# Storing the convolution's parts from ScalarE's queue instead of GpSimd's in a graph network layer

## The chip, the cores and the metric

The kernel runs on one core of a Trainium2 chip. The metric is the device time in microseconds (us) of one execution. A profile is one execution recorded by the hardware profiler; times in it count from the start of its span. The engines are called by their names in the profile: PE is TensorE (matmuls), PEld its weight loads, DVE is VectorE, ACT is ScalarE, POOL is GpSimd and SP is SyncE. The last one computes nothing here: it issues DMA transfers.

## The reference

For each of 32 batches with 512 nodes and 256 channels, the layer normalises `x`, clips it at zero, and computes from the result `h`

```python
hc = relu(bn1(conv1(h)))                 # one tap, 256 to 256 channels
x_conv = relu(bn2(conv2(hc)) + h)        # 17 taps along the nodes
s = h @ w_se.T + b_se                    # 3 numbers per node
A = exp(-squared_distance(s)) * adj
x_nmp = A @ relu(h @ w_msg.T + b_msg)    # messages from the neighbours
# gates of a recurrent cell from [x_conv, x_nmp] and h: r, z, n
out = x + (1 - z) * n + z * h
```

Everything is 32-bit floating point. What matters here is `x_conv`, the convolution of 17 taps with its batch normalisation `bn2`: its values are what the changed stores carry.

## The kernel before, in words

The whole program is written out by a Python planner: there is no loop on the chip. Five generators (`rows`, `begins`, `graphs`, `conv`, `gates`) yield pieces of work; the main loop at the end of the kernel always takes the one whose clock is most behind, and so interleaves their matmuls in one fixed order on PE. The planner keeps an estimated time `now`, and an estimated time `free` for DVE and for ACT. Work that must come a little later than the piece that causes it goes into a list with a due time (`later`, line 158), which the main loop empties as `now` passes. These estimates decide only the order in which instructions stand on each engine. What an instruction waits for is found by the framework from the data that it reads and writes, and from the transfers' completion counters.

The five kinds of work are these:

- `begins`: loads a batch of `x`, normalises it on DVE and ACT, turns it so that channels lie on partitions, and stores it in DRAM as `hd`. From batch 8 on, turning goes by way of DRAM: a store to `xd` (line 928), eight loads that bring it back in blocks (line 907, called from `begin`), and two transposes on DVE into `hT` (line 938), which GpSimd stores to `hd` (line 942).
- `rows`: loads `hT` from `hd` (line 211), multiplies it by the weights of `conv1`, and writes the result to `h1`, the input of the long convolution.
- `conv`: the 17 taps, done as a fast convolution with 25 products for each of seven groups of batches (`STARTS`, line 36). Each product is a sum of matmuls into the PSUM tiles `ps_b` and `ps_c`. DVE prepares the operands (`x`, `xd`) and adds up the products (`n`, `z`, `y`). The weights `w` of the products come from DRAM for each group (line 570).
- `graphs`: masks (`m_sb`, lines 336 and 339), messages and distances, ending in the sums over the neighbours, which ACT copies out of PSUM as `right` and `at`, and which GpSimd stores in DRAM as `nd` (line 170).
- `gates`: for each batch, six products per half of the channels from `hTb` (line 225), `xconv` (line 231) and `xnb` (line 251), which are the batch's `h`, `x_conv` and `x_nmp` loaded again from DRAM, and then the gates on ACT and DVE. The result is added to `res`, a block of `x` (line 907, called from `load_res`), and stored (line 1078).

When the 25 products of a group are summed, `y` holds the group's convolution, and `EVAC` gets an entry for each batch in the group and each half of the channels. `evacuate` (line 677) takes these one at a time: ACT applies `bn2` and brings the columns into order in a tile `part`, of which there are three (line 687), and 0.4 us later by the planner's time a DMA stores it in DRAM, in the batch's `cd` (line 696, the line that the diff changes). From there `load_conv` (line 227) fetches it as `xconv` when the batch's gates are near. A group boundary need not be a batch boundary, so some batches are stored in two pieces. There are 72 parts in all, in seven bursts, one after each group.

DMA transfers are issued by three engines, each in the order of its own instruction stream. SP issues all loads (1254 transfers with a few last stores). GpSimd issues the stores of `hd`, `nd`, `xd`, `out`, of the third weights and, before the change, of `cd` (469 in all). ACT issues 29: the weights' stores at the start (line 561) and some of the last blocks of the output. [...]

Of the kernel before, what the change touches and what calls it, by code (L numbers as in the profile page):

```python
# [48 lines left out]
def kernel(  # L49
# [31 lines left out]
    nc = tc.nc  # L81
# [5 lines left out]
    def sizes(g):  # L87


        nu = STARTS[g + 1] - STARTS[g]  # L90
        return nu, ND * nu, 2 * ND * nu, ND * (nu + 1)
# [39 lines left out]
    dve, act = Engine(nc.vector, 0.12, 0.00108), Engine(nc.scalar, 0.16, 0.0009)  # L131
# [26 lines left out]
    def later(t, f):  # L158
        LATER.append((t, f))
        LATER.sort(key=lambda e: e[0])  # L160
# [28 lines left out]
    CD = {b: dram.tile([P, ND, N], F32, name=f"cd{b}") for b in range(B)}  # L189
# [487 lines left out]
    def evacuate():  # L677

        t, y, g, b, o = EVAC[0]
        if now < t or act.free > now + 0.3 or len(PARTS) > 2 and now < PARTS[-3]:  # L680
            return False
        EVAC.pop(0)
        nu, nh, _, _ = sizes(g)
        v0 = U * b - STARTS[g]
        first, last = max(0, -v0), min(U, nu - v0)
        c = o * nu + v0 + first
        part = late.tile([P, Q * U], F32, name="part", bufs=3)[:, : Q * (last - first)]
        act.activation(
            part.rearrange("p (u h k) -> p k h u", h=2, k=9),
            y.rearrange("p e f (h n) -> p (e f) h n", h=2)[:, :, :, c : c + last - first],  # L690
            AF.Identity, bias=bn2_sh[:, o : o + 1], scale=bn2_sc[:, o : o + 1],
        )
        act.free += 0.7
        PARTS.append(act.free + 5.0)
        n0, n1 = Q * first, min(Q * last, N)
        later(act.free + 0.4, lambda: nc.gpsimd.dma_start(CD[b][:, o, n0:n1], part[:, : n1 - n0]))
        if o == ND - 1 and last == U:
            evacuated[b] = PARTS[-1]
        return True
# [502 lines left out]
    def fill():  # L1202
        while LATER and LATER[0][0] <= now:
            LATER.pop(0)[1]()
        if EVAC:
            evacuate()
        while dve.free < now + 1.5 and background():
            pass
# [159 lines left out]
```

## Time and profile before

| | before |
|---|---|
| time, median of three (lowest to highest) | 2110.38 us (2107.77 to 2115.62) |
| span of the profiled execution | 2111.7 us |
| PE busy | 2058.5 us, 97% |
| DVE busy | 1512.7 us, 72% |
| ACT busy | 754.5 us, 36% |
| POOL busy | 339.9 us, 16% |
| mean granted PE clock | 0.993 |
| bytes moved by DMA | 383.07 MB, 181 GB/s |

Issuing a DMA counts as busy time on POOL, not on the other engines. The profile's view of the DMA issues gives, for each kind of transfer, its issuing engine, its size, and the median time from issue to landing. The ones near the change:

| transfer | issuer | count | KB each | median us to landing |
|---|---|---|---|---|
| `cd<-part`, full parts | POOL | 56 | 256 | 3.3 |
| `hd<-hT` | POOL | 32 | 512 | 5.9 |
| `wd<-w` | ACT | 25 | 512 | 4.2 |
| `xnb<-nd` | SP | 64 | 256 | 3.5 |
| `x_sb<-xd` | SP | 192 | 64 | 3.4 |
| `xconv<-cd` | SP | 32 | 512 | 5.5 |

The other sixteen stores of `cd` carry 81 to 175 KB. One issue of `cd<-part` takes 0.54 us on POOL, and from issue to landing the 72 of them took from 2.3 to 7.8 us.

To read the other views: a line of the waits names the engine and line that waited, what ended the wait, the total in us, the number of times and the longest. A line of the timeline gives the start, the duration, the engine and line, the operation with what it writes and reads, how often it stands in a row, and in brackets the idle time of the engine before it and what ended that.

### The profile page before, as it was taken

What the parts mean: (1) busy time and instruction counts of PE and PEld (TensorE: products, weight loads), DVE (VectorE), ACT (ScalarE), POOL (GpSimd) and SP (SyncE); (2) the same over time, 40 slices, a digit from 0 to 9 for tenths busy, and PEclk for the clock granted to TensorE, in tenths of its full rate; (3) what the DMA queues carried; (4) which work ended last, traced back from release to release, by engine and by line L of the source; (5) the groups of instructions that cost most, each with busy time, mean ns of one, the idle gap of its engine ahead of it and who ended that gap; (6) DMA issues with size and microseconds to landing.
All of it is one profiled execution on the core that took longest, in us unless ns stands there. A gap on an engine that the chain in (4) does not pass through costs nothing.

```text
span 2111.7 us, 25916 instructions
## 1 busy us (share of the span) xinstructions
PE 2058.5 (97%) x8774; PEld 1259.8 (60%) x8774; DVE 1512.7 (72%) x2660; ACT 754.5 (36%) x1267; POOL 339.9 (16%) x582
## 2 busy tenths in 40 slices
PE   9999799999999999999999999999999999999998
PEld 6887476664666556665466665456665666654443
DVE  6887598985898668877488866588985877763333
ACT  5553533226432263332443322533224432233111
POOL 2000112211201021111121101211111110112111
PEclk9999999999999999999999999999999999999999
DMA  7445787776966767676775767677766655624332
GB/s 282 167 149 190 258 252 202 202 206 181 244 186 204 221 170 199 182 184 194 215 185 177 192 189 198 181 185 211 210 177 190 188 155 165 170 72 109 86 90 40
DMA packets 546436, 383.07 MB, mean 181 GB/s; under 512 B 456576, under 2 KB 473472, under 8 KB 545664
## 3 DMA queue, kind: packets, MB, share of 16 engines
q1 hardware_dynamic: 512992, 282.17, 50.7%
q0 software_dynamic: 28624, 86.01, 11.9%
q10 hardware_dynamic: 4688, 13.24, 1.6%
q8 instruction: 70, 1.15, 0.2%
q14 instruction: 62, 0.51, 0.1%
HBM read 281.95 MB, written 99.35 MB: 181 GB/s over the span
## 4 chain that ended last, share of the span: by engine, by line
PE 63%; DMA 1%; issue 1%; DVE 1%; ACT 1%; POOL 0%; SPq 0%; DVEq 0%; ACTq 0%; POOLq 0%
PE ps_acc L136 37%; PE ps_g L136 11%; PE ps_c L136 9%; PE ps_b L136 4%; PE ps_b L867 1%; DMA hT<-hd 1%; ACT r L127 1%; PE ps_g L141 0%; DMA hd<-hT 0%; DMA m_sb<-in_adj_dram 0%; DVE y L127 0%; DVE r L127 0%; ACT at L127 0%; DVE z L127 0%; DVE right L127 0%
## 5 line engine op out<-in xcount | busy, mean ns | idle before, releaser
L136 PE MATMUL ps_acc<-hTb,whh 128*128 128x512 f32 x768 | 359.1, 599 | 18.0 <-ACT r L127 14.6
L136 PE MATMUL ps_acc<-xconv,wih 128*128 128x512 f32 (+1 forms) x772 | 362.0, 591 | 0.0
L136 PE MATMUL ps_acc<-xnb,wih 128*128 128x512 f32 (+1 forms) x772 | 358.9, 591 | 2.8 <-DMA xnb<-nd 2.8
L136 PEld LDWEIGHTS ps_c<-xd,w 128*128 128x128 f32 x2400 | 294.3, 191 | 31.7 <-issue 26.7
L136 PE MATMUL ps_c<-xd,w 128*128 128x135 f32 (+1 forms) x2400 | 303.7, 279 | 0.6 <-DVE z L127 0.3
L1078 POOL DMA_DIRECT2D out_dram<-res x252 | 164.6, 659 | 616.9 <-DVE res L127 520.9
L136 PEld LDWEIGHTS ps_acc<-hTb,whh 128*128 128x128 f32 x768 | 140.4, 190 | 179.8 <-issue 136.9
L136 PEld LDWEIGHTS ps_acc<-xnb,wih 128*128 128x128 f32 x772 | 142.9, 190 | 160.0 <-issue 154.2
L136 PEld LDWEIGHTS ps_acc<-xconv,wih 128*128 128x128 f32 x772 | 142.8, 190 | 156.9 <-issue 154.0
L136 PE MATMUL ps_g<-at,msg 128*128 128x512 f32 x512 | 227.2, 593 | 1.5 <-DVE at L127 1.5
L136 PEld LDWEIGHTS ps_b<-x,w 128*128 128x128 f32 x1200 | 157.0, 190 | 43.3 <-issue 37.3
L127 ACT ACTIVATE mid<-ps_b 128x270 f32<-128x270 f32 (+1 forms) x150 | 59.5, 396 | 344.9 <-PE ps_b L136 334.6
L127 DVE TENSOR_TENSOR r<-ps_acc,r 128x512 f32<-128x512 f32 (+1 forms) x65 | 44.2, 681 | 190.3 <-PE ps_acc L136 190.2
L136 PE MATMUL ps_b<-x,w 128*128 128x135 f32 (+1 forms) x1200 | 163.3, 278 | 0.7 <-ACT at L127 0.7
L136 PEld LDWEIGHTS ps_g<-at,msg 128*128 128x128 f32 x512 | 95.4, 190 | 112.4 <-issue 108.1
L127 DVE SCALAR_TENSOR_TENSOR x<-x,x 128x544 f32<-128x544 f32 (+5 forms) x161 | 137.7, 855 | 2.9
L136 PE MATMUL ps_g<-hT,w 128*128 128x512 f32 (+4 forms) x288 | 122.9, 573 | 15.5 <-DMA hT<-hd 11.5
L127 DVE TENSOR_TENSOR msg<-ps_g,bmsg 128x256 f32<-128x256 f32 x128 | 53.8, 421 | 108.1 <-PE ps_g L136 107.7
L127 ACT ACTIVATE z<-ps_acc,brz 128x512 f32<-128x512 f32 x64 | 44.0, 688 | 234.6 <-PE ps_acc L136 234.5
L127 DVE TENSOR_TENSOR x<-x 128x272 f32<-128x272 f32 (+5 forms) x280 | 127.6, 497 | 0.2
L136 PE MATMUL ps_g<-wmsg,hTg 128*128 128x259 f32 x496 | 124.1, 382 | 0.3 <-DVE aug L127 0.3
L127 DVE TENSOR_TENSOR xd<-x 128x544 f32<-128x544 f32 (+1 forms) x150 | 106.6, 718 | 23.9 <-PE ps_c L136 23.5
(121 smaller groups left out, 2591.9 us busy)
## 6 DMA issues: line engine op xcount, KB each, us to landing
w<-wd SPq DMA_DIRECT2D x125, 768.0 KB, 5.2
m_sb<-in_adj_dram SPq DMA_DIRECT2D x384, 64.0 KB, 3.2
hd<-hT POOLq DMA_DIRECT2D x32, 512.0 KB, 5.9
hT<-hd SPq DMA_DIRECT2D x32, 512.0 KB, 4.6
hTb<-hd SPq DMA_DIRECT2D x32, 512.0 KB, 5.5
xnb<-nd SPq DMA_DIRECT2D x64, 256.0 KB, 3.5
xconv<-cd SPq DMA_DIRECT2D x32, 512.0 KB, 5.5
res<-in_x_dram SPq DMA_DIRECT2D x256, 64.0 KB, 3.0
```

The costliest lines, as they stand in the source:

```text
L127: getattr(self.engine, name)(*tiles, **more)
L136: nc.tensor.matmul(ps, lhsT, rhs, **more)
L867: nc.tensor.matmul(pss[c], gr.left[k, :], gr.right[k, :], start=True, stop=True, tile_position=(32 * c, 0),)
L1078: queue.dma_start(OB[b][:, s.start // 32 : s.stop // 32, o * P + 32 * g : o * P + 32 * g + 32], y[at, s].rearrange("i (k j) -> i k j", j=32),)
```

## The change

The store of each part is issued by ACT, which also computes the part, and no longer by GpSimd:

```diff
         act.free += 0.7
         PARTS.append(act.free + 5.0)
         n0, n1 = Q * first, min(Q * last, N)
-        later(act.free + 0.4, lambda: nc.gpsimd.dma_start(CD[b][:, o, n0:n1], part[:, : n1 - n0]))
+        later(act.free + 0.4, lambda: nc.scalar.dma_start(CD[b][:, o, n0:n1], part[:, : n1 - n0]))
         if o == ND - 1 and last == U:
             evacuated[b] = PARTS[-1]
```

It is meant to take the stores out of GpSimd's queue, where they stand behind stores that wait for other work, and to let the engine that made a part send it off itself. The planner's times are not changed, so PE, DVE and SP keep the order of their instructions; ACT gets 72 DMA issues between its other instructions, and GpSimd loses as many.

## The prediction

> **What bounds the kernel now.** I read the page's first two parts, then the waits of TensorE, ScalarE and GpSimd, then the timeline around the stores that the diff touches. The page's busy row and TensorE's longest waits:
>
> ```profile
> PE 2058.5 (97%) x8774; PEld 1259.8 (60%) x8774; DVE 1512.7 (72%) x2660; ACT 754.5 (36%) x1267; POOL 339.9 (16%) x582
> ...
> PE ps_acc L136 <- ACT r L127: 14.6, 17, 1.8
> PE ps_g L136 <- DMA hT<-hd: 11.5, 5, 6.8
> ```
>
> TensorE is busy for 2058.5 of 2111.7 us; all its gaps together are 53 us. Its order is fixed, so the change can gain at most some gaps and can lose whatever makes a matmul late. GpSimd, which is relieved, is busy for 16%: of its waits, 147.7 us of the stores' own are for the part that they store.
>
> The stores come in bursts of about ten, one at each group's end: in the timeline between 236 and 285 us, then at 497, 752, 1028, 1333, 1624 and 1886. So I read the timeline of two bursts, and one earlier place where ScalarE already stores:
>
> ```profile
> 193.09 0.34 ACTq L561 DMA_DIRECT2D wd<-w  x1
> 193.48 0.56 ACT L127 ACTIVATE z<-ps_c 128x464 f32<-128x464 f32 x1 [0.41 <-ACT w L127]
> ...
> 760.91 0.95 SPq L251 DMA_DIRECT2D xnb<-nd  x2
> 761.96 5.24 SPq L907 DMA_DIRECT2D x_sb<-xd  x8
> 770.50 0.60 ACT L127 ACTIVATE at<-ps_g 128x512 f32<-128x512 f32 x1 [2.84 <-PE ps_g L136]
> 770.99 3.53 ACT L127 ACTIVATE part<-y,bn_shift,bn_scale 128x522 f32<-128x522 f32 x3
> 772.54 0.70 DVE L127 STREAM_TRANSPOSE hT<-x_sb 128x512 f32<-128x512 f32 x1
> 775.45 1.88 PE L136 MATMUL ps_acc<-xnb,wih 128*128 128x512 f32 x4
> ...
> 1342.97 3.78 PE L136 MATMUL ps_acc<-hTb,whh 128*128 128x512 f32 x4 [1.80 <-ACT r L127]
> 1359.80 7.43 SPq L907 DMA_DIRECT2D x_sb<-xd  x8
> 1368.21 0.70 DVE L127 STREAM_TRANSPOSE hT<-x_sb 128x512 f32<-128x512 f32 x1
> 1372.18 0.70 DVE L127 STREAM_TRANSPOSE hT<-x_sb 128x512 f32<-128x512 f32 x1
> 1373.18 0.54 POOL L942 DMA_DIRECT2D hd<-hT  x1 [1.17 <-DVE hT L127]
> 1373.49 0.69 ACT L127 ACTIVATE z<-ps_acc,brz 128x512 f32<-128x512 f32 x1 [2.32 <-PE ps_acc L136]
> 1383.27 1.40 PE L136 MATMUL ps_g<-hT,w 128*128 128x171 f32 x8 [0.33 <-DMA hT<-hd]
> ```
>
> Columns: start, time, engine, line, operation; in brackets the idle time before it. Note two things. SyncE's loads of `xnb` and `x_sb` are issued ten to fifteen microseconds before ScalarE makes the parts beside them: today SyncE runs ahead. And 1359.80 to 1383.27 is one chain: load of `x_sb`, two transposes, store to `hd`, load of `hT`, matmul, with 0.33 us of waiting left at its end.
>
> [...]
>
> **The change part by part.** *Removed:* 72 stores from GpSimd, 72 x 0.54 = 39 us of its time, none on TensorE's path: no matmul waits for GpSimd after the first microseconds. The `hd` store at 1373.18 waited for VectorE, not for a store ahead of it. I count 0.
>
> *Added on ScalarE:* 72 issues. Each leaves the engine idle for about 0.40 us (0.40 and 0.41 after the two stores at 187.82 and 193.09): 72 x 0.40 = 29 us into 1357 us of idle time. It matters only where ScalarE works without a pause up to something that TensorE awaits. That is so in the first burst: TensorE waits 0.67 us at 263.81 for the exponentials, and four stores now stand before them: 4 x 0.40 = 1.6 us. Elsewhere bursts end in idle time of 1 to 5 us: 0 to 1 us together.
>
> *Added waits.* This is the part that the diff does not show. I compared the two built programs, instruction by instruction with the semaphores that each awaits. The orders of TensorE, VectorE and SyncE are unchanged. But the DMAs of SyncE and ScalarE share eight completion counters, given out in turn, and each DMA first waits until the previous one on its counter has landed; GpSimd's have eight of their own. Moving 72 stores over makes them take turns with SyncE's loads, in both directions.
>
> Stores behind loads: for each store I compared the landing of the DMA before it on its counter with the time at which ScalarE arrives there. All 72 had landed, by 2.5 to 47 us. Nothing is added.
>
> Loads behind stores: 60 of SyncE's DMAs now wait for a part's store, and SyncE, held at one, holds all those behind it. Where SyncE ran ahead, this costs. Landing of a store: 3.3 us, the median of the 56 stores of 256 KB on GpSimd; of `xnb` 3.5 and `x_sb` 3.4.
>
> Burst at 752: the first `xnb` load follows a store that ScalarE reaches after `at` at 770.50 and two parts, some 2.43 us later: 773.4. It lands at 776.8, the `xnb` load at 776.8 + 3.5 = 780.3, and TensorE wants it at 775.45: **+4.8 us**. Next come eight loads of `x_sb`, behind two stores at about 774.8 (landed 778.1). The fourth, at 0.65 us each (5.24 for eight), lands at about 783.5, and VectorE, which needs it at 772.54, stands for 11 us. What is queued there: the sums of the next products, a read of `ps_c` at 781.46 among them, which TensorE needs only at 787.79, or 792.6 once it is itself 4.8 late. VectorE's own idle time of 2.2 us at 780.15 takes part of the 11, so this second delay hides: 0.
>
> Burst at 1333: the fourth of the eight `x_sb` loads follows a store that stands on ScalarE behind `z`, which awaits TensorE and ends at 1374.2. Landed at 1374.2 + 3.3 = 1377.5; four more loads at 0.65 and a landing of 3.4 put the eighth at 1383.5. The second transpose started at 1372.18: 11.3 us late, and the chain to the matmul at 1383.27 has no slack: **+11.3 us**. From both sides: with the shortest store landing, 2.3 us, it is 10; with the longest, 7.8, 16.
>
> Burst at 236: the last of eight `x_sb` loads follows a store after `right` (ends 261.95, now 1.6 later): landed 266.9, load landed at 270.3 to 272.1 against 269.68. The transpose and, 1.8 us behind it, the read of `ps_c` that TensorE awaits at 272.32 come up to 2.4 us later; with the 1.6 above, which overlaps, **+2.5 us**. Bursts at 497 and 1886: the `hT` load is 5.7 us late with 5.9 to spare, two `xnb` loads about 2.5 late with 3.2 to spare: **+1 us** together. At 1028 and 1624 the delayed loads keep 4 us or more: 0.
>
> Last, after a gap TensorE ran slower: the four matmuls at 1342.97 took 3.78 us instead of 1.88. For two new long gaps: 2 x 1.9 = **+3.8 us**.
>
> Sum: 4.8 + 11.3 + 2.5 + 1 + 3.8 = 23.4; 2110.4 + 23.4 = 2134 us.
>
> **The rivals.** (a) *All hidden*: the stores land earlier than I think, or SyncE is held by something else anyway. Then only the first burst's 1.6 us and a little more remain: 2113 us. For it: SyncE's large waits at other places (314.1 us for `ps_c`). Against it: at 761 and 1354 it issues without waiting. (b) *It spreads*: ScalarE's issue time lies wholly on the path (29 us: 2139), or a late load makes the next stores late, they the next loads, and a second pair of such gaps opens: 2134 + 16 + 5 = 2155. Against it: ScalarE is busy for 36%, and bursts last only 40 to 57 us. (c) *Faster*: freed from its queue, the stores and those behind them on GpSimd go out earlier. A part's buffer came late three times (3.8 us), the `xnb` wait of 2.8 us and an `hT` wait of 3.3 us could go with it: 2111 - 7 = 2103 us. Against it: the waits of those two loads' stores were for ScalarE, not for a store ahead.
>
> **How the numbers follow.** Forecast 0.64, (a) 0.17, (b) 0.15, (c) 0.04. The forecast and (b) are slower by over 0.5% (10.6 us), and a quarter of (a) is: 0.64 + 0.15 + 0.05 = 0.84; no difference 0.12; faster 0.04. The range starts at (a)'s 2113, for half of that case, and ends at 2152, which takes in the 16 us of the long landing (+4.7) and most of (b). Left out: 0.04 + 0.08 + 0.06.
>
> **What would show it.** In the profile after: in SyncE's waits, lines 339, 251 and 907 waiting for landings of `cd<-part`, ten and more microseconds long near 761 and 1354; a wait of `ps_acc` for `xnb<-nd` of about 5 us near 776; one of `ps_g` for `hT<-hd` of about 11 near 1390; idle ScalarE of 0.4 us behind each store. I am wrong if SyncE issues the `x_sb` loads before the parts' stores as now, if ScalarE stands waiting for loads, or if TensorE's gaps do not grow in those two bursts.

## The result, and the profile after

| | before | after |
|---|---|---|
| median of four runs (lowest to highest) | 2110.74 us (2107.77 to 2115.62) | 2126.15 us (2123.58 to 2129.63) |
| span of the profiled execution | 2111.7 us | 2127.9 us |
| PE busy | 2058.5 us | 2063.4 us |
| POOL busy | 339.9 us | 298.6 us |
| bytes moved by DMA | 383.07 MB, 181 GB/s | 383.07 MB, 180 GB/s |

The change makes the kernel slower: the ratio is 1.0072, with a 95% interval from 1.0048 to 1.0096, or +15.4 us. The forecast was +23.4 us (2134 us).

The busy row of the page after the change:

```profile
PE 2063.4 (97%) x8774; PEld 1262.5 (59%) x8774; DVE 1512.6 (71%) x2660; ACT 757.9 (36%) x1267; POOL 298.6 (14%) x510
```

GpSimd got its 41 us back, and nobody needed them. PE's span grew by 16.2 us, its busy time by only 4.9: two thirds of the loss are gaps. The longest waits of TensorE after the change:

```profile
PE ps_acc L136 <- ACT r L127: 15.5, 17, 2.3
PE ps_g L136 <- DMA hT<-hd: 15.3, 4, 7.0
PE ps_acc L136 <- DVE r L127: 6.4, 4, 2.9
PE ps_acc L136 <- DMA xnb<-nd: 6.3, 2, 5.1
```

The waits for `hT` grew from 11.5 to 15.3 us and those for `xnb` from 2.8 to 6.3; the row for VectorE's `r` was 3.5 us. ScalarE's row is hardly longer. Where the loads are held is seen in SyncE's own waits after the change (line of the waiting DMA, what it waited for, total, times, longest):

```profile
SPq L907 <- DMA cd<-part: 21.0, 13, 4.1
SPq L339 <- DMA cd<-part: 17.5, 6, 4.9
SPq L251 <- DMA cd<-part: 12.2, 3, 8.0
SPq L225 <- DMA cd<-part: 5.7, 1, 5.7
```

None of these four rows exists before the change. Three shorter ones (lines 570, 231 and 211: 4.5, 4.5 and 1.9 us) are left out. The loads of `x_sb`, masks, `xnb` and `hTb` do not read `cd` and have no data in common with a part; of all seven lines only 231 reads `cd`.

That the counters tie them together can be read from the traces directly, because each DMA's record names its counter (the views above do not print it). Before the change SyncE's 1254 and ScalarE's 29 DMAs name the same eight counters (100 to 102 and 104 to 108), and GpSimd's 469 name eight others (111 to 118); after it the same eight serve 1254 and 101, the others 397. The records fit a fixed cycle through the eight: all 1283 DMAs of SyncE and ScalarE before, all 1355 after. In each trace 1736 DMAs have another before them on their counter. None was issued before that one had landed; the closest followed it by 0.016 us. In the trace after the change, 60 of SyncE's DMAs have a part's store as the DMA before them on their counter, and 27 of the 60 were issued within 0.1 us after that store had landed. One of them is the first `xnb` load of the burst at 752: it was issued at 774.76, on the counter of the store issued at 772.66, which had landed at 774.70.

The timeline of the burst at 752, after the change:

```profile
764.70 2.03 SPq L339 DMA_DIRECT2D m_sb<-in_adj_dram  x4
770.80 0.60 ACT L127 ACTIVATE at<-ps_g 128x512 f32<-128x512 f32 x1 [2.84 <-PE ps_g L136]
771.29 2.43 ACT L127 ACTIVATE part<-y,bn_shift,bn_scale 128x522 f32<-128x522 f32 x2
772.66 0.33 ACTq L696 DMA_DIRECT2D cd<-part  x1
774.76 0.84 SPq L251 DMA_DIRECT2D xnb<-nd  x2
776.89 8.92 SPq L907 DMA_DIRECT2D x_sb<-xd  x8
780.97 3.48 PE L136 MATMUL ps_acc<-xnb,wih 128*128 128x512 f32 x4 [5.06 <-DMA xnb<-nd]
785.80 0.71 DVE L127 STREAM_TRANSPOSE hT<-x_sb 128x512 f32<-128x512 f32 x1 [12.88 <-DMA x_sb<-xd]
```

Before, the `xnb` loads went out at 760.91 and the `x_sb` loads at 761.96. Now SyncE stands 8.0 us in front of `xnb`, until the store issued at 772.66 has landed, and TensorE stops for 5.06 us. The held loads held those behind them too: the DMA before the third `x_sb` load on its counter had landed at 767.22, but that load went at 781.49, 0.37 us after the second, which a store had held until 781.11. VectorE stops for 12.88 us as well, but that wait hides, as the forecast said: TensorE falls no further behind in the 200 us that follow (7.12 us at 778.10 in the table below, 6.08 at 1370.27).

The burst at 1333, after the change:

```profile
1374.65 6.16 SPq L339 DMA_DIRECT2D m_sb<-in_adj_dram  x4
1379.57 0.69 ACT L127 ACTIVATE z<-ps_acc,brz 128x512 f32<-128x512 f32 x1 [3.64 <-PE ps_acc L136]
1379.63 0.33 ACTq L696 DMA_DIRECT2D cd<-part  x1
1380.92 4.62 SPq L907 DMA_DIRECT2D x_sb<-xd  x8
1385.32 0.71 DVE L127 STREAM_TRANSPOSE hT<-x_sb 128x512 f32<-128x512 f32 x1 [10.94 <-DMA x_sb<-xd]
1387.32 0.71 DVE L127 STREAM_TRANSPOSE hT<-x_sb 128x512 f32<-128x512 f32 x1 [0.92 <-DMA x_sb<-xd]
1388.33 0.57 POOL L942 DMA_DIRECT2D hd<-hT  x1 [15.84 <-DVE hT L127]
1390.59 2.84 PE L136 MATMUL ps_acc<-hTb,whh 128*128 128x512 f32 x4 [2.93 <-DVE r L127]
1395.06 0.34 SPq L211 DMA_DIRECT2D hT<-hd  x1
1398.87 2.62 PE L136 MATMUL ps_g<-hT,w 128*128 128x171 f32 x8 [5.43 <-DMA hT<-hd]
```

This is the chain named in the prediction, and it now decides: load, two transposes, `hd` store, `hT` load, matmul. The late transposes cost TensorE twice. First `r`, which stands behind them on VectorE, comes 2.93 us late; then `hT` comes 5.43 us late.

### Where the 16 us lie

Both traces have the same 8774 matmuls in the same order, so the start of the same matmul can be subtracted. The shift (after minus before) along the run:

| place (time before) | shift | change over the stretch |
|---|---|---|
| before the burst at 236, at 236.28 | +0.35 | +0.4 |
| after the burst at 236, at 272.32 | +0.45 | +0.1 |
| behind the `xnb` wait near 566 (2.77 us before, 1.22 after), at 570.29 | -1.38 | -1.8 |
| before the late `xnb`, at 774.16 | +0.30 | +1.7 |
| after the four matmuls at 775.45, at 778.10 | +7.12 | **+6.8** |
| before the burst at 1333 bites, at 1370.27 | +6.08 | -1.0 |
| after the `hT` matmuls at 1383.27 and the slow ones behind them, at 1390.27 | +17.05 | **+11.0** |
| at 1617.97, and then to the end | +16.18 | -0.9 |

Two bursts hold 17.8 us of the loss; all the rest of the run gives back 1.6. In that rest there are steps of another kind: stretches of 3.41 us in which the traces show a granted PE clock of 0.50. By an estimate from these two numbers each costs 3.41 x 0.50 = 1.7 us. The one at 490.03 before the change has its counterpart at 497.29 after it, and the one at 743.04 after the change, which makes the +1.7 of the fourth row, has none before, where the clock is 1.00 from 493.45 to 1039.58.

### The profile page after: what moved, and what is told of

The parts are those of the page before. It is cut to its first block, busy times and chain, and to the rows that moved or that the text cites. A ratio compares the mean times of both kernels' runs of the same rounds, so it can differ in the third digit from the quotient of the medians.

```text
span 2127.9 us, 25834 instructions
## 1 busy us (share of the span) xinstructions
PE 2063.4 (97%) x8774; PEld 1262.5 (59%) x8774; DVE 1512.6 (71%) x2660; ACT 757.9 (36%) x1267; POOL 298.6 (14%) x510
## 2 busy tenths in 40 slices
DMA packets 551427, 383.07 MB, mean 180 GB/s; under 512 B 456576, under 2 KB 475392, under 8 KB 550656
## 3 DMA queue, kind: packets, MB, share of 16 engines
q8 instruction: 70, 1.15, 0.2%
## 4 chain that ended last, share of the span: by engine, by line
PE 61%; issue 2%; DVE 2%; DMA 2%; ACT 1%; POOL 0%; DVEq 0%; POOLq 0%; SPq 0%
PE ps_acc L136 36%; PE ps_g L136 11%; PE ps_c L136 9%; PE ps_b L136 4%; PE ps_b L867 1%; DMA hT<-hd 1%; DVE y L127 0%; ACT r L127 0%; DMA xnb<-nd 0%; PE ps_g L141 0%; DMA hd<-hT 0%; DVE z L127 0%; DVE r L127 0%; POOL out_dram L1078 0%; DMA out_dram<-res 0%
## 5 line engine op out<-in xcount | busy, mean ns | idle before, releaser
L136 PE MATMUL ps_acc<-hTb,whh 128*128 128x512 f32 x768 | 359.5, 599 | 21.9 <-ACT r L127 15.5
L136 PE MATMUL ps_g<-hT,w 128*128 128x512 f32 (+4 forms) x288 | 125.0, 582 | 19.3 <-DMA hT<-hd 15.3
```

The source lines that it names most:

```text
L136: nc.tensor.matmul(ps, lhsT, rhs, **more)
```

## The experiments

The theory is the prediction's: SyncE's loads take turns with ScalarE's stores on the completion counters, and a store that ScalarE reaches late holds the loads behind it. The rivals: ScalarE's time for the issues; the part's 256 KB, which now travel beside SyncE's loads; the number of transfers or the shifted order of the counters as such. Each time is the median of 6 to 22 executions. The kernel before took 2110.73 us beside e1 to e4 and 2111.18 beside e5 to e9.

| run | us | ratio (95% interval) | against before |
|---|---|---|---|
| e1: ScalarE stores in the bursts at 752 and 1333 only | 2127.57 | 1.0077 (1.0061 to 1.0094) | +16.8 |
| e2: ScalarE stores in the other five bursts only | 2109.43 | 0.9995 (0.9986 to 1.0004) | -1.3 |
| e9: in the burst at 1333 only | 2121.62 | 1.0052 (1.0034 to 1.0070) | +10.4 |
| e8: in the bursts at 497, 1028, 1624 and 1886 only | 2109.53 | 0.9993 (0.9981 to 1.0005) | -1.7 |
| e3: stores on GpSimd, ScalarE's time spent twice over | 2117.86 | 1.0032 (1.0019 to 1.0044) | +7.1 |
| e4: stores on GpSimd, small stores by ScalarE | 2122.52 | 1.0054 (1.0039 to 1.0070) | +11.8 |
| e5: stores on GpSimd, small stores by SyncE | 2113.82 | 1.0011 (1.0002 to 1.0020) | +2.6 |
| e7: stores on GpSimd, small stores of the part by ScalarE | 2130.39 | 1.0090 (1.0072 to 1.0108) | +19.2 |

### Which bursts cost: e1, e2 and e9

The groups are numbered from 0; group 2 ends in the burst at 752, group 4 in the one at 1333. The edit of e1 against the kernel before; e2 has the two engines exchanged, and e9 has `g == 4` for the condition:

```diff
-        later(act.free + 0.4, lambda: nc.gpsimd.dma_start(CD[b][:, o, n0:n1], part[:, : n1 - n0]))
+        later(act.free + 0.4, lambda: (nc.scalar if g in (2, 4) else nc.gpsimd).dma_start(CD[b][:, o, n0:n1], part[:, : n1 - n0]))
```

e1:

> Only the stores of the third and fifth group (22 of the 72, the bursts near 752 and 1333 us) go out on ScalarE, the other 50 stay on GpSimd. Theory (SyncE's loads wait, on the shared completion counters, for ScalarE's stores, and this costs only in these two bursts): all of the loss or a little more, +15 to +18 us, with a wait of ps_acc for xnb of about 5 us near 776 and the matmul behind the hT load 8 us or more later near 1390. Rival 1 (ScalarE's issue time) and rival 2 (the stores' own transfers cost more from this queue): in proportion to the stores, 22/72 of 15.4 = +4.7 us.

e2:

> The other half of the same cut: the 50 stores of the five other groups go out on ScalarE, those of the third and fifth group stay on GpSimd. Theory: about nothing, -2 to +1 us, since in these bursts the held loads have time to spare and the xnb wait near 565 us got 1.5 us shorter in the changed kernel. Rivals 1 and 2: 50/72 of 15.4 = +10.7 us.

e9:

> ScalarE stores the parts of the burst at 1333 us alone, GpSimd all others. Theory: this burst's own cost by the chain of late x_sb loads, transposes, hd store, hT load and matmul: +8 to +11 us and up to 2 us of slowed matmuls, 2119 to 2123 us; no wait for xnb over 3 us at 775. Rival (the two bursts act together, the second is late only because the first was): 0 to +4 us, 2111 to 2115 us.

e1 costs +16.8 us and e2 gains 1.3; together +15.5, which is the whole change's +15.4. So 22 of the 72 stores cost everything, and the other 50 nothing that can be told from noise. e9 gives +10.4, so +6.4 is left for the burst at 752, which fits the 11.0 and 6.8 of the shifts above. The two bursts are independent: e9's trace keeps the same stops in the burst at 1333 though nothing was late before it.

From the longest waits of TensorE in e9:

```profile
PE ps_g L136 <- DMA hT<-hd: 13.7, 4, 5.5
PE ps_acc L136 <- DVE r L127: 6.4, 4, 2.9
...
PE ps_acc L136 <- DMA xnb<-nd: 2.4, 1, 2.4
```

The 5.5 us for `hT` and the 2.9 us for `r` are there, the 5.1 us for `xnb` is not.

### ScalarE's time: e3

The stores stay on GpSimd; at each of the 72 places ScalarE makes two extra copies of a scratch tile, 144 of 0.353 us, 51 us in all, where the 72 issues were put at 29 us.

```diff
-    nc.gpsimd.memset(mhalf, -0.5)
+    nc.gpsimd.memset(mhalf, -0.5); scr = const.tile([P, 180], F32, name="scr"); nc.gpsimd.memset(scr, 0.0)
...
-        later(act.free + 0.4, lambda: nc.gpsimd.dma_start(CD[b][:, o, n0:n1], part[:, : n1 - n0]))
+        later(act.free + 0.4, lambda: (nc.gpsimd.dma_start(CD[b][:, o, n0:n1], part[:, : n1 - n0]), [nc.scalar.activation(scr, scr, AF.Copy) for _ in range(2)]))
```

> All stores stay on GpSimd; where a store would have been issued on ScalarE, ScalarE instead copies a small tile of 128x180 onto itself twice, which adds some 0.4 to 0.7 us of its time at the same 72 places (29 to 50 us in all) and no DMA. The added copies compute nothing that is used. Theory: 0 to +2 us, for ScalarE's time at these places is mostly idle time. Rival 1 (issue time): +15 us or more. Rival 2: 0.

It measured +7.1 us: more than the theory's 0 to 2, less than the rival's 15. ScalarE's time is not free. But the loss lies elsewhere: in the burst at 236 (+3 us) and near 566 (+5 us, of which 2.6 are gone again by 1043). Near 566 TensorE waits 5.3 us in all for `xnb` (2.8 before); where the rest of the 5 us comes from, and that ScalarE's copies made these loads late, is not shown. The wait for `right` in the burst at 236, from the timeline of e3:

```profile
264.03 0.73 ACT L696 ACTIVATE scr<-scr 128x180 f32<-128x180 f32 x2
264.19 0.69 PE L867 MATMUL ps_b<-right,left 5*128 5x512 f32 x1 [2.35 <-ACT right L127]
```

Before, that wait was 0.82 us, and after the change it is 1.17. In the burst at 752 the trace of e3 has no wait for `xnb`, and in the one at 1333 it waits 0.76 us for `hT`. So 51 us of extra work on ScalarE make neither of the two stops that the change makes.

### The counters alone: e4, e5 and e7

In these three the parts are still stored by GpSimd. Beside each, an extra small transfer (16 bytes per partition, 2 KB) goes to a spare tile in DRAM and takes a turn on the shared counters. In e4 ScalarE stores a constant; in e5 SyncE stores it instead; in e7 ScalarE stores the first bytes of the part, and so waits for the part like the real store. The edit of e4:

```diff
-    nc.gpsimd.memset(mhalf, -0.5)
+    nc.gpsimd.memset(mhalf, -0.5); spare_d = dram.tile([P, 80, 4], F32, name="spare_d")
...
-        later(act.free + 0.4, lambda: nc.gpsimd.dma_start(CD[b][:, o, n0:n1], part[:, : n1 - n0]))
+        later(act.free + 0.4, lambda k=len(PARTS): (nc.gpsimd.dma_start(CD[b][:, o, n0:n1], part[:, : n1 - n0]), nc.scalar.dma_start(spare_d[:, k], mhalf)))
```

e5 has `nc.sync.dma_start(spare_d[:, k], mhalf)` there, e7 `nc.scalar.dma_start(spare_d[:, k], part[:, :4])`.

e4:

> All stores stay on GpSimd; beside each, ScalarE issues a store of 16 bytes a partition from a constant tile to a spare place in DRAM. It takes a turn on the shared counters and ScalarE's issue time, but carries no data of the convolution. The spare stores compute nothing that is used. Theory: nearly the whole loss, +11 to +16 us, a little less than the change because these tiny stores should land about 1 us sooner, with the same waits for xnb and hT in the same two bursts. Rival 1 with its issue time: also +15, but spread, without those waits. Rival 2: 0 to +1 us.

e5:

> The parts' stores stay on GpSimd; beside each, SyncE stores 16 bytes per partition of a constant to a spare tile in DRAM. These small stores take the shared completion counters in turn as ScalarE's did in the run before, 72 of them at the same places of the program, but they stand in SyncE's own stream and wait for nothing that ScalarE makes. Theory (a load is late because its counter's turn is held by a store that ScalarE reaches late): SyncE only spends 72 x about 0.4 us = 29 us more, nearly all of it while it runs ahead; 0 to +1 us, 2111 to 2112 us, no wait of TensorE for xnb over 3 us in the burst at 752, and at most 1 us for hT at 1383. Rival (the number of small transfers, or a counter order shifted by 72, is what costs): about as much as with ScalarE's small stores, +8 to +12 us.

e7:

> The parts' stores stay on GpSimd; beside each, ScalarE stores the first 16 bytes per partition of the part itself to a spare tile in DRAM. Against ScalarE's small stores of a constant, the only difference is that the small store waits for the part, as the real store does; against the changed kernel, the 256 KB go by GpSimd's queue and counters. Theory: the small store goes out when the part is ready, at about 772.7 in the burst at 752, lands 2.4 us later at 775.1, and the xnb load lands 3.5 us behind it at 778.6: TensorE stands 3 us there where the constant's store made it stand 0.5; burst at 1333 as with the constant's store, 6.5 us, or up to 10 us. In all 2110.7 + 12 to + 17 = 2123 to 2128 us. Rival (the burst at 752 costs what it does only because the part's 256 KB from ScalarE share the DMA engines with the xnb load): 752 stays at 0.5 us and the whole at 2122.5.

SyncE's waits in e4 show the same hold as the change, by transfers of 2 KB that nobody reads and that landed in a median of 2.4 us (the full parts' stores before: 3.3):

```profile
SPq L907 <- DMA spare_d<-mhalf: 13.4, 8, 4.0
SPq L339 <- DMA spare_d<-mhalf: 12.7, 5, 5.3
SPq L231 <- DMA spare_d<-mhalf: 8.4, 3, 4.1
SPq L251 <- DMA spare_d<-mhalf: 7.3, 2, 6.0
```

e4 costs +11.8 us. By the shift of the same matmuls, 9.5 of it lie in the burst at 1333 (2.30 us of waiting for `r`, 4.52 for `hT`, and slow matmuls behind them: the four behind `r` took 3.21 us, four of the same kind at 1380.38 had taken 1.88) and 2.0 in the burst at 236. In the burst at 752 less than 0.5 us is lost: the constant is ready early, the small stores go at 772.26 and 772.71, and the `xnb` loads at 773.72, a microsecond sooner than in the change; the first of them lands in 3.2 us instead of 6.2.

e5 has just as many small transfers at the same places of the program, and costs +2.6 us: somewhat more than the 0 to 1 expected, far from the rival's 8 to 12. In its timeline SyncE issues near its old times:

```profile
761.54 0.57 SPq L696 DMA_DIRECT2D spare_d<-mhalf  x1
762.21 2.03 SPq L339 DMA_DIRECT2D m_sb<-in_adj_dram  x4
764.33 1.07 SPq L251 DMA_DIRECT2D xnb<-nd  x2
...
1361.75 2.56 SPq L696 DMA_DIRECT2D spare_d<-mhalf  x2
1364.55 4.18 SPq L907 DMA_DIRECT2D x_sb<-xd  x8
```

The `xnb` loads go at 764.33, not at 774.76; the `x_sb` loads at 1364.55, not at 1380.92. The shift of TensorE's matmuls is the same before and after each of the two bursts, within 0.1 us. So neither the number of transfers nor the shifted turns cost much: 2.6 us of e4's 11.8. What costs is that the turn before a load belongs to a transfer of another engine which comes late: 58 of SyncE's DMAs stand behind one of ScalarE's small stores on their counter in e4, and none in e5.

e7 costs +19.2 us, more than the expected 12 to 17 and more than the change itself, though only 2 KB of each part travel by ScalarE's queue. The burst at 752 in its timeline:

```profile
776.00 2.43 ACT L127 ACTIVATE part<-y,bn_shift,bn_scale 128x522 f32<-128x522 f32 x2
...
777.38 0.33 ACTq L696 DMA_DIRECT2D spare_d<-part  x1
...
779.70 0.83 SPq L251 DMA_DIRECT2D xnb<-nd  x2
...
783.44 3.11 PE L136 MATMUL ps_acc<-xnb,wih 128*128 128x512 f32 x3 [2.82 <-DMA xnb<-nd]
```

Waiting for the part makes the small store late, and with it the load: TensorE stops for 2.82 us (3 expected), where the constant's store had cost nearly nothing. The shift grows by 4.7 us in this burst and by 9.8 in the one at 1333 (the 6.5 expected there had left out the slow matmuls). That is 14.5 of the change's 17.8, with the data still on GpSimd: the part's 256 KB in ScalarE's queue can account for at most the rest. What e7 loses besides lies ahead of these two bursts, 3.6 us of it in the burst at 236: there a `part` waits 1.91 us (0.24 before) until GpSimd's store has freed its buffer, and the exponentials stand behind it.

What is left over in the burst at 752 is in the `xnb` load itself. From the store's issue to the matmul the change takes 780.97 - 772.66 = 8.3 us, e7 783.44 - 777.38 = 6.1. Of the 8.3, the store takes 2.1 and the load 6.2; in e1, where ScalarE stores the parts of this burst too, the split is 3.5 and 4.5, with the sum 8.0. The two transfers may be slower because they run among the parts' own; that was not tested by itself, and where these 2 us come from stays open.

### A choice of bursts: e8

```diff
-        later(act.free + 0.4, lambda: nc.gpsimd.dma_start(CD[b][:, o, n0:n1], part[:, : n1 - n0]))
+        later(act.free + 0.4, lambda: (nc.scalar if g in (1, 3, 5, 6) else nc.gpsimd).dma_start(CD[b][:, o, n0:n1], part[:, : n1 - n0]))
```

> ScalarE stores the parts of the bursts at 497, 1028, 1624 and 1886 us; GpSimd those of the three at 236, 752 and 1333. Theory: nothing is late by a counter in those four but what has slack; the earlier nd store near 565 that was seen when GpSimd was relieved stays: -1 to -3 us, 2108 to 2110 us, with the wait for xnb near 566 at 1.2 to 1.5 us instead of 2.8. Rival (gain near 565 was chance, and ScalarE's issues cost): 2111 to 2113 us.

2109.53 us is 1.7 less than before, and the interval of the ratio still holds 1. In the trace the wait for `xnb` near 566 fell from 2.77 to 0.62 us. If there is a gain it is under 0.2%; it is no version to prefer with certainty.

## Why the prediction was right, step by step

**The mechanism was right.** The step "Moving 72 stores over makes them take turns with SyncE's loads" is shown by SyncE's new rows, by the counters in the trace, and by e4, e5 and e7. The rate of the bytes hardly changed with the issuer: 181 GB/s before, 180 after. The time did: in this kernel the issuing engine decides whose transfers wait for whose, and that made 15.4 us.

**"Stores behind loads: nothing is added" was right.** Each of the 72 stores was issued 1.8 to 46.7 us after the DMA before it on its counter had landed (the forecast had 2.5 to 47), and TensorE's longest row of waits for ScalarE grew by 0.9 us.

**Burst at 752: +4.8 forecast, a wait of 5.06 measured.** The path was right; that the number came so near was luck, for two errors cancelled. The store was put at 773.4 and taken to land in 3.3 us; it went at 772.66, beside the second part's computation, and landed within 2.1. The load was taken to land in 3.5 us and took 6.2. The delayed `x_sb` loads hid, as forecast.

**Burst at 1333: +11.3 forecast, and 13.2 with the slower matmuls; measured 9.5, and 11.0 with them.** The path was right: the fourth `x_sb` load was issued at 1383.11, just after the store at 1379.63, the one before it on its counter, had landed (1383.09). Three sizes in the sum were too large. ScalarE issued that store 0.06 us after `z` had begun, not at `z`'s end; the four loads behind it followed about 0.5 us apart, not 0.65; and the last of them landed in 2.2 us, not 3.4. So the second transpose came not 11.3 but 1387.32 - 1372.18 - 6.1 (the shift by then) = 9.0 us late, and the matmul behind it 9.5. It was also a close race, which the prediction did not see: until 1380.50 SyncE had been held at the masks by two other stores, which took 4.7 and 5.6 us to land. From the pace of the loads, about 0.5 us apart, I estimate that without the store behind `z` the fourth load would have gone only 0.5 us sooner. The prediction also missed that VectorE, held by the transposes, would make `r` late. That wait of 2.93 us came first and took its share of the later one, so the sum did not grow.

**Burst at 236: +2.5 forecast, +0.1 measured.** The term was mis-sized. The exponentials came 0.9 us later (264.04 against 263.16), not 1.6; and though the last `x_sb` load was issued 2.2 us later (266.49 against 264.31), the second transpose ran at 269.70 (before 269.68), so it landed in time.

**Bursts at 497 and 1886: +1 forecast, none found.** The `hT` load at 503.36 went at 508.26, its matmuls at 513.28 ran at 513.48: it was late as forecast and had the slack.

**Slower matmuls: 3.8 us forecast, about 3 measured** (1.6 behind the `xnb` wait, 1.5 in the burst at 1333). The stretches of time after the change show it. Columns: stretch, its length, busy time of PE, PEld, DVE, ACT and POOL with the number of instructions, granted PE clock, DMA share, GB/s.

```profile
777.00:779.00 2.00, 0.00 (x0) 0.00 (x0) 0.00 (x0) 0.00 (x0) 0.00 (x0) 1.00 0.90 280
779.00:781.00 2.00, 0.03 (x1) 0.03 (x1) 0.00 (x0) 0.00 (x0) 0.00 (x0) 0.90 0.57 170
781.00:783.00 2.00, 2.00 (x3) 0.97 (x4) 0.00 (x0) 0.00 (x0) 0.00 (x0) 0.50 0.41 68
```

TensorE stands idle for 5.06 us, and when the work comes back at 780.97 the granted clock is 0.50, by the trace's clock records from 780.59 to 784.00. Shorter gaps stand before such stretches too. In the burst at 1333 the clock is 0.50 from 1391.58 to 1401.82, and it falls there after a gap of 2.93 us. And the same short gap was followed by half clock in one execution and not in the other (first before the change, then after it):

```profile
744.45 2.84 PE L136 MATMUL ps_g<-hT,w 128*128 128x512 f32 x6 [1.16 <-ACT at L127]
743.09 4.50 PE L136 MATMUL ps_g<-hT,w 128*128 128x512 f32 x6 [1.15 <-ACT at L127]
```

The clock granted from 743 to 745 us is 1.00 before and 0.51 after. So the length of one gap does not settle in these traces whether the clock is halved.

**GpSimd's relief: 0 forecast, 1 to 2 us measured.** This is rival (c)'s argument, and it was there in small: the wait for `xnb` near 566 fell to 1.22 us after the change, to 1.50 in e2 and to 0.62 in e8, and in the runs in which GpSimd stores the parts of the burst at 497 it is 2.0 (e4) to 5.3 us (e3) in all. The prediction named this wait under the rival and left the gain out of its sum. (The rival's 2111 - 7 is 2104, not 2103; nothing hangs on it.) In the time of the whole kernel the gain is not shown: the intervals of e2 and e8 hold 1.

**The other rivals.** (a), all hidden, falls with the two stops. (b), a spread, falls with e1, e2 and e9: their parts add up to the whole, and e9 has the second pair of gaps without the first. ScalarE's issue time on the path falls with e2, where 50 of the issues cost nothing.

Forecast minus measured, with the slower matmuls in their bursts: 752 -0.1, 1333 +2.2, 236 +2.4, and +2.7 for the two quiet bursts and the rest of the run, the chance stretches of half clock among it. That is the 7.2 us between the 23.4 forecast and the 16.2 of the profiled execution.

## What to carry to other kernels

Before moving a DMA to another engine's queue, look at what the two engines share: here it was eight completion counters given out in turn, and loads with no tie to the moved stores waited for them, one for 8.0 us. SyncE, which issued the first `xnb` load of the burst at 752 ten microseconds before ScalarE began the part beside it (760.91 against 770.99), lost that lead when its turns were mixed with those of an engine that issues when its computation is done: the load went at 774.76. In this kernel it paid to keep the late issuer and the early one on different counters: the same parts stored on GpSimd's counters left that load at 760.91 (2110.74 us in all against 2126.15). A queue that looks cheap to relieve (GpSimd, 16% busy) was no gain by itself: it got 41 us back, and the kernel took 15.4 us longer. The price was read on the queue that received the work and on SyncE's, which shares its counters.

## What the runs showed that was not expected

- A store of 2 KB that nobody reads can cost as much as one of 256 KB: 72 of them on ScalarE's queue cost 11.8 us (e4) or 19.2 us (e7), on SyncE's 2.6 us (e5); the change's own 72 stores, 56 of them of 256 KB, cost 15.4 us.
- ScalarE issues a DMA while it still computes: after the change one store went out at 1379.63, 0.06 us after a `z` of 0.69 us had begun, and one at 772.66, while the second of two `part`s ran (771.29 to 773.72 together). Counting the first from the end of `z` put it too late: it does not need that result.
- A gap of 1.15 us on TensorE was followed by 3.41 us at a granted clock of 0.50 in one execution, and one of 1.16 us before the same matmuls by 1.00 in another. The six matmuls behind it took 4.50 and 2.84 us, a difference of 1.7.
- From the issue of the same `xnb` load to the start of the matmul that waited for it passed 3.7 us in e7, 4.5 in e1 and 6.2 after the change.
